# A turn of attention on one Trainium2 core: the order of a unit's scores, projections, sums and transpositions

## The chip, the cores and the metric

The kernel runs on one core of a Trainium2 chip. The core has a matrix engine (TensorE, PE in the profile; PEld are its weight loads), a vector engine (VectorE, DVE), an engine for activation functions (ScalarE, ACT), a general engine (GpSimd, POOL) and an engine that issues most of the copies (SyncE, SP). The engines run side by side; each works through its own queue in order, and semaphores make one wait for another. TensorE writes its results into PSUM, eight banks of 128 x 512 f32 numbers, and VectorE and ScalarE read them from there.

The metric is the device time of one launch in microseconds (us). The profile shows one execution, instruction by instruction. Its span is from the first to the last instruction.

## The reference

Three layers are computed on 16 batches of 512 tokens, 256 wide: half a feed-forward layer, an attention layer, half a feed-forward layer again, each added to its input. The change touches the attention layer alone:

```python
b, s, e = x.shape                        # 16, 512, 256; x is layer-normalized
q = x @ Wq + bq
kv = x @ Wkv + bkv
k, v = jnp.split(kv, [H * DQK], axis=-1) # H = 16 heads, DQK = DV = 64
q = _rope(q.reshape(b, s, H, DQK).transpose(0, 2, 1, 3))
k = _rope(k.reshape(b, s, H, DQK).transpose(0, 2, 1, 3))
scores = jnp.einsum('bhqd,bhkd->bhqk', q, k) * (1.0 / np.sqrt(DQK))
scores = jnp.where(causal[None, None], scores, -jnp.inf)
probs = jax.nn.softmax(scores, axis=-1)
out = jnp.einsum('bhqk,bhkd->bhqd', probs, v)
return out @ Wo + bo                     # heads beside each other again
```

All is f32.

## The kernel before

The program has three stages: the first feed-forward layer, attention, and the second feed-forward layer. Attention works on *units*: a batch and a group of four heads, 64 units in all, four to a batch. It is a loop over turns, `for u in range(-2, nu)`. A turn works on several units at once, each at another step: it makes q and k of unit u+3 (`queries_keys`), the scores and the softmax weights of unit u+2 (`new`), the values of unit u+1 (`values`, p_v), and the weighted sums (`sums`, p_av) and the output projection (`leave`, p_ay) of unit u. In this loop the queues of all engines hold the instructions in the order in which the program's lines issue them (`manual_schedule`). So the order of the calls is the order of the work.

The 512 tokens of a unit are four tiles of 128 queries. Tile i needs (i+1) x 128 keys, because of the causal mask. The steps:

- `Rotated.half` and `add`: p_q and p_k, each in two halves of 128 x 512. VectorE multiplies each half by the cosine and by the sine (four instructions for q, four for k), POOL adds and subtracts.
- `exps(tiles)`: scores p_as. Four heads stand in four groups of 32 rows of TensorE's array, and each head has a PSUM bank. VectorE reads each bank (L853: scale, mask and the row's minimum of the negated scores, amn), ScalarE exponentiates (L857) and sums the row (ars). Tile 3, tile 2, and tiles 1 and 0 together are three calls. Tiles 3 and 2 stand in the buffer pr0, tiles 1 and 0 in pr1.
- `normalize(tiles)`: VectorE's reciprocal of the sums (L862), then POOL scales the weights (L865).
- `turn_most(0..3)`, `turn_corner`, `turn_rest`: VectorE transposes the weights in blocks of 32 x 32 from pr into sq (L880), five instructions for tiles 3 and 2 and two for tiles 1 and 0.
- `move`: SP issues 16 copies of 160 KB (L903) from sq into prT, which put the blocks of 32 into the right partitions. sq and prT have one buffer each.
- `values`: p_v in two halves on the whole 128 x 128 array; ScalarE copies them out (L809).
- `sums`: p_av, two calls of two heads; each head uses 64 columns of the array. It reads prT. ScalarE copies the result out with a bias (oT, L940).
- `leave`: p_ay on the whole array, two calls; VectorE adds them to x (L953). After a batch's last head group SP copies x out.

At every fourth turn a new batch begins: `enter` normalizes its tokens on ScalarE (L759) and adds the output bias to x on POOL (L762), and `width` transposes them on TensorE (p_ahT, L769; ScalarE copies the two halves into ahT, L770), which p_q, p_k and p_v read. Once in two batches `spread` takes a square root on ScalarE, for which a table of functions is loaded and then the exponential's again.

TensorE's order in a turn before is: sums, (width), scores 3, p_v, p_q, scores 2, p_k, p_v, scores 1 and 0, p_ay. The four `turn_most` and the corner of a unit stand at the end of the turn that made its weights. `turn_rest` and the copies stand in the next turn, behind the sums.

All PSUM tiles take the eight banks in rotation: a tile waits until the one eight before it has been read.

## Time and profile before

| | us |
|---|---|
| median of 3 runs | 2398.57 |
| lowest and highest | 2395.6 and 2398.81 |
| the profiled execution | 2397.34 |
| its span | 2395.6 |
| attention in it | about 475 to 1994 |
| one turn, TensorE's sums to the next sums | 23.77; 24.80 where a batch begins |
| busy in one turn of 23.78: PE, DVE, ACT, POOL | 23.78, 20.42, 11.48, 13.15 |

A row of a group or of the timeline gives the start or the busy time in us, the engine, the line of the kernel, the operation, the output and inputs by their names in the program, and the number of instructions; what stands in brackets is the idle time before it and what ended it. In the chain, a row is the start, the length and the work that the end of the program had to wait for. Ends of matmuls are modelled in the profile, and neighbouring ones overlap by a little.

### The profile page before, as it was taken

Reading aid. Unit: us, or ns where it says so; the run is one execution under the profiler, and the core shown is the slowest. Engines: PE = TensorE matmul, PEld = TensorE weight load, DVE = VectorE, ACT = ScalarE, POOL = GpSimd, SP = SyncE. Lnnn points to the kernel's source line nnn. Section 1 sums busy time; section 2 is a strip of 40 time slices with the busy share of each in tenths; the row PEclk is TensorE's granted clock in tenths of the full one; section 3 lists DMA queues with packets and bytes.
Section 4 is the critical chain, followed back from the end, with each engine's and each line's share of the span. In section 5 each row is a group of like instructions: output and inputs, shape, how many; then the busy total and the mean of one; then the engine's idle time right before and its main releaser. Section 6 shows DMA issues by size and latency. Waiting matters only on the chain.

```text
span 2395.6 us, 42393 instructions
## 1 busy us (share of the span) xinstructions
PE 2334.5 (97%) x14696; PEld 1468.1 (61%) x14696; DVE 1771.7 (74%) x4669; ACT 1072.4 (45%) x2924; POOL 1067.4 (45%) x1692
## 2 busy tenths in 40 slices
PE   7999889899999999999999999999999999999899
PEld 5765479455565655555555555555555566765488
DVE  8542278788888888888888888888888865542287
ACT  4333233355455555545545545555555453323233
POOL 2220044555564655565646555556555542210043
PEclk9999999999999999999999999999999999999999
DMA  9009942245454545464645454646454545019734
GB/s 319 12 2 372 365 117 71 45 106 124 103 127 107 123 112 119 106 132 97 133 105 124 105 125 98 136 94 139 100 126 103 126 104 187 1 54 383 302 111 137
DMA packets 141709, 320.56 MB, mean 134 GB/s; under 512 B 36980, under 2 KB 84152, under 8 KB 133304
## 3 DMA queue, kind: packets, MB, share of 16 engines
q1 hardware_dynamic: 140908, 317.31, 49.7%
q8 instruction: 117, 1.92, 0.3%
q14 instruction: 96, 0.79, 0.1%
q10 hardware_dynamic: 588, 0.54, 0.1%
HBM read 135.84 MB, written 16.78 MB: 64 GB/s over the span
## 4 chain that ended last, share of the span: by engine, by line
PE 85%; DVE 3%; DMA 2%; ACT 2%; issue 1%; POOL 0%; SPq 0%; DVEq 0%; ACTq 0%; POOLq 0%
PE p_as L845 13%; PE p_av L933 12%; PE p_v L806 9%; PE p_ay L949 9%; PE p_k L784 9%; PE p_q L784 9%; PE p_cy L661 4%; PE p_cq L369 4%; PE p_cs L630 2%; PE p_z L480 2%; PE p_u L522 2%; PE p_ds L449 2%; DMA w<-in_e_Wg_dram 1%; PE p_catT L651 1%; PE p_y L549 1%; PE p_vw L619 1%
## 5 line engine op out<-in xcount | busy, mean ns | idle before, releaser
L865 POOL TENSOR_SCALAR pr<-pr,ars 128x512 f32<-128x512 f32 (+3 forms) x1024 | 525.0, 537 | 653.7 <-DVE ars L862 653.7
L857 ACT ACTIVATE pr<-pr,amn 128x512 f32<-128x512 f32 (+3 forms) x1024 | 561.5, 549 | 462.1 <-DVE amn L853 462.0
L853 DVE CUSTOM_DVE_ANT_0 pr<-p_as,causal 128x512 f32<-128x512 f32 (+3 forms) x1024 | 434.3, 484 | 97.8 <-PE p_as L845 96.3
L880 DVE STREAM_TRANSPOSE sq<-pr 128x768 f32<-128x768 f32 x441 | 375.7, 906 | 13.5 <-issue 12.3
L845 PE MATMUL p_as<-k,q 32*128 32x512 f32 (+3 forms) x4096 | 332.5, 449 | 3.6 <-POOL k L795 3.6
L933 PE MATMUL p_av<-prT,v 128*64 128x512 f32 (+3 forms) x2048 | 291.7, 438 | 7.2 <-DVE ars L862 6.3
L845 PEld LDWEIGHTS p_as<-k,q 32*128 32x128 f32 x4096 | 180.1, 185 | 131.8 <-issue 51.9
L806 PEld LDWEIGHTS p_v<-wv,ahT 128*128 128x128 f32 x1024 | 189.3, 190 | 98.5 <-issue 45.8
L806 PE MATMUL p_v<-wv,ahT 128*128 128x256 f32 x1024 | 248.4, 386 | 0.0
L933 PEld LDWEIGHTS p_av<-prT,v 128*64 128x64 f32 x2048 | 140.0, 137 | 164.8 <-issue 134.1
L949 PE MATMUL p_ay<-wo,aoT 128*128 128x256 f32 x1024 | 238.7, 386 | 0.3 <-ACT aoT L940 0.3
L784 PE MATMUL p_k<-ahT,wk 128*128 128x512 f32 x512 | 236.9, 605 | 0.0
L784 PE MATMUL p_q<-ahT,wq 128*128 128x512 f32 x512 | 230.5, 592 | 0.2 <-ACT ahT L770 0.2
L949 PEld LDWEIGHTS p_ay<-wo,aoT 128*128 128x128 f32 x1024 | 189.1, 190 | 32.0 <-ACT aoT L940 1.1
L857 ACT ACTIVATION_READ_ACCUMULATOR pr<-pr,amn 128x1 f32 x1024 | 191.4, 187 | 0.0
L784 PEld LDWEIGHTS p_k<-ahT,wk 128*128 128x128 f32 x512 | 92.1, 189 | 126.2 <-issue 115.9
L940 ACT ACTIVATE aoT<-p_av,bcol 128x512 f32<-128x512 f32 x128 | 88.0, 687 | 181.1 <-PE p_av L933 181.1
L784 PEld LDWEIGHTS p_q<-ahT,wq 128*128 128x128 f32 x512 | 97.1, 190 | 95.8 <-issue 86.6
L608 POOL TENSOR_TENSOR kbd<-kT,own 128x256 f32<-128x256 f32 x32 | 19.7, 619 | 290.1 <-DVE kT L575 253.0
L661 PE MATMUL p_cy<-vw,catT 128*128 128x256 f32 x512 | 122.7, 384 | 3.0 <-ACT catT L653 3.0
L480 PE MATMUL p_z<-atT,h 128*128 128x256 f32 x512 | 120.2, 389 | 3.9 <-ACT atT L471 3.9
L809 ACT COPY v<-p_v 128x512 f32<-128x512 f32 x128 | 73.5, 574 | 104.3 <-PE p_v L806 104.3
(157 smaller groups left out, 3292.0 us busy)
## 6 DMA issues: line engine op xcount, KB each, us to landing
prT<-sq SPq DMA_DIRECT2D x1008, 160.0 KB
w<-in_e_W_dram SPq DMA_DIRECT2D x64, 1024.0 KB
w<-in_e_Wg_dram SPq DMA_DIRECT2D x32, 1024.0 KB
out_dram<-x SPq DMA_DIRECT2D x64, 256.0 KB
xl<-in_attn_x_dram SPq DMA_DIRECT2D x16, 512.0 KB
xl<-out_dram SPq DMA_DIRECT2D x16, 512.0 KB
x<-in_attn_x_dram SPq DMA_DIRECT2D x15, 512.0 KB
wq<-in_attn_Wq_dram SPq DMA_DIRECT2D x16, 64.0 KB
```

Source lines behind the costliest of these rows:

```text
L369: nc.tensor.matmul(pq, w["c_Wq"][:, k, c * P:(c + 1) * P], hTs[b][:, k, :], start=(k == 0), stop=(k == NC - 1))
L480: nc.tensor.matmul(pz[:, c * 256:(c + 1) * 256], h[:, t, c * P:(c + 1) * P], atT[:, t, :], start=(t == 0), stop=(t == NT - 1))
L661: nc.tensor.matmul(py[:, t * D:(t + 1) * D], atT[:, c, t * P:(t + 1) * P], vws[b][:, c, :], start=(c == 0), stop=(c == NC - 1))
L784: nc.tensor.matmul(pq, self.w[:, k, at:at + P], hTs[self.b][:, k, :], start=(k == 0), stop=(k == NC - 1))
L806: nc.tensor.matmul(pv[:, t * 256:(t + 1) * 256], hTs[b][:, k, (t0 + t) * P:(t0 + t + 1) * P], wv[:, k, hg * HG * DQ:(hg + 1) * HG * DQ], s ...
L845: nc.tensor.matmul(banks[j][:, at:at + w], q[n][j * 32:(j + 1) * 32, i * P:(i + 1) * P], k[n][j * 32:(j + 1) * 32, :w], start=(n == 0), st ...
L853: nc.vector.tensor_tensor_reduce(out=self.at(i, j), in0=banks[j][:, at:at + w], in1=causal[:, S - w:], scale=-1.0 / math.sqrt(DQ), scalar= ...
L857: nc.scalar.activation(self.at(i, j), self.at(i, j), AF.Exp, bias=self.mn[:, i, j:j + 1], scale=-1.0, accum_out=self.rs[:, i, j:j + 1])
L865: nc.gpsimd.tensor_scalar(self.at(i, j), self.at(i, j), self.rs[:, i, j:j + 1], 1.0, ALU.mult, ALU.mult)
L880: nc.vector.transpose(view(self.sq, j * blocks * SQ + dst[0] * SQ, [(blocks * SQ, nh)] + [(s * SQ, n) for s, (_, n) in zip(dst[1:], of)] + ...
L933: nc.tensor.matmul(po[j * DQ:(j + 1) * DQ, :].rearrange("d (a f) -> d a f", a=NSQ)[:, :, t * SQ:], vs[u][:, t, head * DQ:(head + 1) * DQ], ...
L949: nc.tensor.matmul(py[:, t * D:(t + 1) * D], oTs[u][:, pair, (t0 + t) * P:(t0 + t + 1) * P], wo[:, hg * (HG // 2) + pair, :], start=(pair ...
```

## The change

Calls in the turn change their places; what is computed stays as it was.

- TensorE's order becomes: sums, scores 3, p_v, (width), p_v, p_q, p_k, p_ay, scores 2, scores 1 and 0. `queries_keys` is not cut in pieces any more, and `leave` comes before scores 2.
- VectorE turns a unit's weights in one go in the turn after the one that made them: `turn_most(0)`, the reciprocal of tiles 1 and 0, `turn_most(1..3)`, the corner and the rest, and then the copies are issued. The reciprocal of tile 2 stands halfway in the reads of tiles 1 and 0 (`halfway`).
- `enter` moves to the start of the turn that needs it, ahead of the sums; the addition of the output bias is split off (`with_bias`) and follows the scaling of tiles 1 and 0 on POOL.
- `width` moves from ahead of scores 3 to between the two halves of p_v.
- `spread` moves ahead of `leave` and scores 2.
- In the last turns of the loop the last unit's scaling and its transpositions on TensorE (`turn_at_once`) move likewise; `normalize` is called `scaled`.

```diff
+        def with_bias(b):
             for t in range(NT):
                 nc.gpsimd.tensor_tensor(xs[b][:, t, :], xs[b][:, t, :], row, ALU.add)
...
-            def exps(self, tiles):
+            def exps(self, tiles, halfway=None):
...
                 for j in range(HG):
+                    if halfway and j == HG // 2:
+                        halfway()
...
-            def normalize(self, tiles):
+            def scaled(self, tiles):
...
                 old = ws.get(u + 1)
-                if old and u + 2 == nu:
+                fresh = u + 3 < nu and units[u + 3][1] == 0
+                if fresh:
+                    enter(units[u + 3][0])
+                if u + 2 == nu:
+                    old.scaled((1, 0))
                     values(u + 1, 0)
                     values(u + 1, 2)
-                    old.turn_at_once()
                 if u >= 0:
                     sums(u, 0)
                     sums(u, 1)
-                if old and u + 2 < nu:
+                if old and u + 2 == nu:
+                    old.turn_at_once()
+                elif old:
+                    old.turn_most(0)
+                    old.scaled((1, 0))
+                    old.turn_most(1)
+                    old.turn_most(2)
+                    old.turn_most(3)
+                    old.turn_corner()
                     old.turn_rest()
                     old.move()
+                if fresh:
+                    with_bias(units[u + 3][0])
                 if u + 4 in stds:
                     scales((u + 4) // (PB * NHG), stds.pop(u + 4))
-                if u + 3 < nu and units[u + 3][1] == 0:
-                    width(units[u + 3][0])
                 if new:
                     new.exps((3,))
...
                 if new:
-                    new.normalize((3,))
+                    new.scaled((3,))
                 if 0 <= u + 1 < nu - 1:
                     values(u + 1, 0)
-                for one in qk[:2]:
+                if fresh:
+                    width(units[u + 3][0])
+                if 0 <= u + 1 < nu - 1:
+                    values(u + 1, 2)
+                for one in qk:
                     one()
+                if 0 <= u + 5 < nu and (u + 5) % (PB * NHG) == 0:
+                    stds[u + 5] = spread((u + 5) // (PB * NHG))
+                if u >= 0:
+                    leave(u, 0)
+                    leave(u, 2)
                 if new:
                     new.exps((2,))
-                for one in qk[2:3]:
-                    one()
-                if new:
-                    new.normalize((2,))
-                for one in qk[3:]:
-                    one()
-                if 0 <= u + 1 < nu - 1:
-                    values(u + 1, 2)
-                if 0 <= u + 5 < nu and (u + 5) % (PB * NHG) == 0:
-                    stds[u + 5] = spread((u + 5) // (PB * NHG))
-                if new:
-                    new.exps((1, 0))
-                if u >= 0:
-                    leave(u, 0)
-                if new:
-                    new.normalize((1, 0))
-                turns = new and u + 3 < nu
-                if turns:
-                    new.turn_most(0)
-                    new.turn_most(1)
-                if u >= 0:
-                    leave(u, 2)
-                if turns:
-                    new.turn_most(2)
-                    new.turn_most(3)
-                    new.turn_corner()
-                if u + 4 < nu and units[u + 4][1] == 0:
-                    enter(units[u + 4][0])
+                    new.exps((1, 0), lambda: new.scaled((2,)))
```

More of the change, by code (lines that the diff above doesn't have):

```diff
@@ L968, in attention @@
         enter(0)
+        with_bias(0)
         ap = yield [lambda: width(0)] + queries_keys(0)
```

## The prediction

> **What bounds the kernel now.** I read the page's first part, the chain, one turn in the chain's order of time, that turn on the other engines, and last a turn that was late.

> ```profile
> PE 2334.5 (97%) x14696; PEld 1468.1 (61%) x14696; DVE 1771.7 (74%) x4669; ACT 1072.4 (45%) x2924; POOL 1067.4 (45%) x1692
> ...
> PE 85%; DVE 3%; DMA 2%; ACT 2%; issue 1%; POOL 0%; SPq 0%; DVEq 0%; ACTq 0%; POOLq 0%
> ```

> TensorE is the bound. The attention stage (475 to 1994 us) is 64 units; its steady turns are nearly all TensorE:

> ```profile
> 1223.24 4.46 PE p_av L933 x32
> 1227.69 1.93 PE p_as L845 x16
> 1229.62 1.92 PE p_v L806 x8
> 1231.55 3.43 PE p_q L784 x8
> 1234.98 1.50 PE p_as L845 x16
> 1236.48 3.63 PE p_k L784 x8
> 1240.12 1.73 PE p_v L806 x8
> 1241.84 1.52 PE p_as L845 x32
> 1243.36 3.65 PE p_ay L949 x16
> ```

> See the same work at two prices: p_v 1.92 after scores, 1.73 after p_k; p_k 3.63 after scores, the same shape as p_q (3.43, after p_v); p_ay 3.65 after scores, as much as two p_v (3.46). About 0.2 us goes at each change between 32-row scores, 64-column sums and whole-array work. There are seven changes in a turn; a turn takes 23.77 us, one that starts a new batch (four more transposes to each half, p_ahT) 24.80. The clock is granted at 1.00 there.

> The other engines in that turn:

> ```profile
> 1223.78 0.20 DVE L862 RECIPROCAL ars<-ars 128x8 f32<-128x8 f32 x1 [1.26 <-ACT pr L857]
> 1226.87 4.13 DVE L880 STREAM_TRANSPOSE sq<-pr 128x768 f32<-128x768 f32 x5
> 1224.08 3.23 POOL L865 TENSOR_SCALAR pr<-pr,ars 128x256 f32<-128x256 f32 x8 [2.62 <-DVE ars L862]
> 1234.53 0.56 ACT L809 COPY v<-p_v 128x512 f32<-128x512 f32 x1
> ```

> VectorE's last transposition of a unit ends at 1231.0, 7.5 us after the sums began (1223.2); sixteen copies (sq to prT) follow, and the next sums need them all. How close that is shows in a turn after a square root (two table loads on ScalarE), where VectorE was 1.5 us later:

> ```profile
> 765.91 4.53 PE L933 MATMUL p_av<-prT,v 128*64 128x512 f32 x32
> 786.04 3.72 PE L949 MATMUL p_ay<-wo,aoT 128*128 128x256 f32 x16
> 790.04 2.23 PE L933 MATMUL p_av<-prT,v 128*64 128x512 f32 x13 [0.28 <-issue]
> 770.75 4.13 DVE L880 STREAM_TRANSPOSE sq<-pr 128x768 f32<-128x768 f32 x5
> ```

> The windows around its end (columns: stretch, its length, busy PE, PEld, DVE, ACT, POOL, clock, DMA share, GB/s):

> ```profile
> 789.00:789.50 0.50, 0.50 (x4) 0.33 (x2) 0.05 (x1) 0.50 (x4) 0.50 (x1) 1.00 0.05 21
> 789.50:790.00 0.50, 0.26 (x2) 0.00 (x0) 0.00 (x0) 0.50 (x3) 0.27 (x1) 1.00 0.00 0
> ```

> Transpositions end at 774.9, the copies move bytes until after 789.0, TensorE stands idle and starts at 790.04: 15.1 us after the last transposition. The chain names it "issue", but the copies are what it had to wait for. So the copies are hidden in an ordinary turn by little more than 1 us.

> **The change, step by step.**

> *Fewer changes of shape on TensorE.* A turn becomes sums, scores 3, then p_v, p_v, p_q, p_k, p_ay together, then scores 2 and 1/0 together. Three changes go: p_k at p_q's 3.43 (0.20), p_ay at 3.46 (0.19), scores 1/0 0.20 less (1.32; it has scores 2's column count, and no row shows it after scores, so I take the same 0.2; ends 0 and 0.24). TensorE's own turn: 4.46+1.93+1.92+1.73+3.43+3.43+3.46+1.50+1.32 = 23.18, that is 0.59 less. Over some 62 turns, 37 us, if nothing else waits.

> *What lies between a unit's last scores and its sums.* Before, from the end of scores 1/0 to the sums that need them there are p_ay and a whole turn, 3.65+23.77 = 27.4 us. After, p_ay has moved ahead of the scores, and only one turn is left: 23.18 us. What must pass in it, from the end of scores 2 (0): VectorE starts tile 2 at once, ScalarE 0.59 behind it (1213.23, 1213.82) and exponentiates four heads at a pitch of 0.60, so by 3.0 it takes tiles 1 and 0, now queued right behind; these take 3.62 (1220.13 to 1223.75): 6.65. VectorE has by then read them, done the reciprocal of tile 2 and turn_most(0) (about 5.7), and stands at the reciprocal of tiles 1/0, which waits for ScalarE. POOL begins 0.30 after that reciprocal and scales for 3.23: 10.3 with a handover. VectorE's other three turn_most and the corner (3×0.88+0.58) run beside it and are no later. The last two transpositions, which need POOL, take 1.8: 12.1. Scores 1/0 end 1.3 after scores 2, so the last transposition stands 10.8 us after the last scores. The nearest row is the chain of before, 11.1 (scores end 1195.7, transpositions 1206.9); bounds 10.0 (POOL's last heads overlap the first of the two) and 11.8 (VectorE late at the scores, and the 0.2 to 0.55 idle ahead of a first transposition on the path). With 15.1 of copies (the late turns, among them those that begin at 958.51 and 1536.33, show 14.9 to 15.3): 25.9 against a cover of 23.18. The sums are late by 2.72. turn_most(0) now also waits until the copies of the unit before have left sq, and all of VectorE's turn is queued behind it; they have landed when the late sums begin, 2.72 after the scores, and VectorE comes to it at about 3.6, so I take nothing for it (0.9 of cover; later copies would add their excess to the chain).

> The wait is shared by two turns: lateness of one start delays nothing in the chain measured from the scores before it. So two plain turns take 23.18+25.9 = 49.1 us, against 47.5 before.

> The late turn measured 15.1 us for the copies, at 205 to 208 GB/s. [...]

> *A new batch.* `width` moves from just after the sums to behind the first p_v; its two ScalarE copies (ahT) now stand behind the four exponentials of tile 3 and p_v's copy, and p_q needs them. The exponentials wait for VectorE to read scores 3, which stands behind all transpositions. Before: last transposition 1206.87, p_v's copy from 1210.40, 3.5 later; add 0.57 for it and 0.53 for the first ahT: 4.65 after the last transposition (two copies took 1.06). After, that is 10.8−2.72+4.65 = 12.7 from the start of the sums. TensorE is ready for p_q at 4.46+1.93+1.92+1.03+1.73 = 11.07. It waits 1.66 (bounds: 0, if ahT comes earlier than I think; 4.4, where the sums were not late).

> *The rest, at nothing.* enter stands ahead of the sums' evictions on ScalarE (2.06 us): TensorE doesn't need these banks until p_q. with_bias (2.8 us of POOL) follows the scaling, with POOL idle until tile 3's reciprocal; without that cover it would delay p_k's rotation. The square root and its table loads now stand ahead of p_ay, where ScalarE waits for scores 2 anyway; the late turns (0.24 and 0.36 us over; 1.0 the most) go, 2.4 us in all. p_ay's two adds on VectorE now stand ahead of its reads of scores 2; p_ay ends 1.5 before these do and an add takes 0.65, so they wait for nothing unless VectorE is behind (third rival). SP's queue: the outputs' copies stay behind the sixteen, none passes another, and the sixteen start after the sums' end at 4.5 as before. PSUM: p_k takes the banks of scores 3, the first two read by 11.5 and 12.1 of a turn; p_k starts at 13.5.

> *Sum.* Of four turns one starts a batch: 23.18+1.03+1.66 = 25.87; then no wait (the copies had time), a wait, none, a wait: a block is 25.87+25.9+23.18+25.9 = 100.85 us. Before: 24.80+3×23.77 = 96.11. 15 blocks × 4.74 = 71.1, less 2.4 = 69 us. The profiled execution took 2397.34 us (span 2395.6), 1.2 under the median of 2398.57: 2397.3+69 = 2466.

> **Rivals.** Under 0.2% (5 us) counts as no change.

> *TensorE never waits (faster).* Then 37+2.4 us go: 2358. For it: the 0.2 us are plain in the rows. It needs last transpositions no later than 8.1 after the scores for the copies, and 6.4 for ahT. Against it: ScalarE alone is busy until 5.35 after the scores, and POOL and VectorE follow by semaphore. The block breaks even where the last transposition comes 8.5 after the scores. I give 0.07, and 0.03 to no change.

> *One of the two waits isn't there.* Without ahT's wait, 15×1.66 = 25 less: 2441. With the chain at its lower bound, 10.0: 2×0.8×15 = 24 less: 2442; both: 2417. Chance 0.22.

> *VectorE becomes the bound.* It is busy 20.4 of 23.8 us, and now its reads of p_ay come just ahead of scores 2: stats, q, k and p_ay end at about 22 in a turn, when scores 2 end. Late by 1 us, or copies or chain at their upper ends (2×(1.0+0.2)×15 = 36): 2502. Chance 0.08.

> **How the numbers follow.** The forecast holds 0.60 between 2442 and 2500. 2466 is its value. Range 2417 to 2500: out go the faster and the equal case (0.10) and the part beyond 2500 (0.08). Slower in all but the first rival: 0.90; same 0.03; faster 0.07.

> **What would show it.** Right: TensorE idle some 2 to 3 us ahead of p_av in every second turn, or 1.4 in each; the last transposition 8 to 11 after the start of the sums; some 1.7 idle ahead of p_q in every fourth turn; p_k near 3.43 and p_ay near 3.46. Wrong: p_av back to back with the scores (the copies or the chain are shorter than taken), p_q waiting 4 us or not at all, or scores 2 waiting for banks (VectorE the bound).

## The result, and the profile after

The changed kernel takes 2484.76 us (median of 4 runs, 2475.49 to 2492.17), the kernel before beside it 2397.6 (4 runs, 2395.6 to 2398.81). The ratio is 1.036, with a 95% interval of 1.0325 to 1.040: 87 us slower. 2466 was forecast, with a range of 2417 to 2500. The profiled execution is the longest of the four, 2492.17 us with a span of 2490.4.

The page after, shares of the span by engine, and the head of the chain:

```profile
PE 2344.9 (94%) x14696; PEld 1519.3 (61%) x14696; DVE 1789.0 (72%) x4669; ACT 1049.7 (42%) x2924; POOL 1066.4 (43%) x1692
...
PE 72%; ACT 8%; DVE 6%; DMA 3%; SPq 2%; issue 2%; POOL 1%; DVEq 0%; ACTq 0%; POOLq 0%
```

TensorE was 85% of the chain, now it is 72%, and ScalarE (8%, it was 2%), VectorE and the copies have taken the rest. TensorE is busy 10 us longer than before (2344.9 us against 2334.5), and its idle time has grown by 84 us, from 61 to 146. Here is a turn that starts a batch and the plain one behind it, on TensorE (start, length, and in brackets the idle time before):

```profile
1219.41 4.53 PE L937 MATMUL p_av<-prT,v 128*64 128x512 f32 x32 [1.77 <-DVE ars L866]
1223.87 2.00 PE L847 MATMUL p_as<-k,q 32*128 32x512 f32 x16
1225.80 1.99 PE L808 MATMUL p_v<-wv,ahT 128*128 128x256 f32 x8
1227.63 1.04 PE L771 MATMUL p_ahT<-ident,h 128*128 128x128 f32 x8
1228.50 1.89 PE L808 MATMUL p_v<-wv,ahT 128*128 128x256 f32 x8
1232.44 3.70 PE L786 MATMUL p_q<-ahT,wq 128*128 128x512 f32 x8 [2.04 <-ACT ahT L772]
1235.98 3.60 PE L786 MATMUL p_k<-ahT,wk 128*128 128x512 f32 x8
1239.41 3.62 PE L953 MATMUL p_ay<-wo,aoT 128*128 128x256 f32 x16
1242.96 2.88 PE L847 MATMUL p_as<-k,q 32*128 32x384 f32 x48
1245.77 4.53 PE L937 MATMUL p_av<-prT,v 128*64 128x512 f32 x32
...
1271.50 4.53 PE L937 MATMUL p_av<-prT,v 128*64 128x512 f32 x32 [2.50 <-DVE amn L857]
...
1294.67 4.53 PE L937 MATMUL p_av<-prT,v 128*64 128x512 f32 x32
```

Both forecast gaps are there. The sums (p_av) of every second turn are late, by 1.77 and 2.50 here, and not those between (1245.77 and 1294.67 follow the scores at once). In a new batch's turn p_q waits 2.04 for ahT. The gain is there too: from 1271.50 to 1294.67 a turn without a wait takes 23.17 us, where 23.77 were needed.

The label of the gap ahead of p_av, "DVE amn", names the engine whose semaphore came last by the profile. What TensorE had to have are the copies; the chain has them ahead of the sums at 1271.50, until 1271.30:

```profile
1265.80 5.50 DMA prT<-sq
```

VectorE's rows of the turn from 1245.77, and the windows behind them (columns: stretch, length, busy PE, PEld, DVE, ACT, POOL, clock, DMA share, GB/s):

```profile
1251.20 0.20 DVE L866 RECIPROCAL ars<-ars 128x8 f32<-128x8 f32 x1 [1.36 <-ACT pr L861]
1251.32 4.96 DVE L884 STREAM_TRANSPOSE sq<-pr 128x768 f32<-128x768 f32 x6
```

```profile
1258.00:1268.00 10.00, 10.00 (x56) 6.31 (x58) 8.81 (x20) 2.84 (x8) 7.61 (x8) 1.00 0.98 217
...
1270.50:1271.00 0.50, 0.00 (x0) 0.00 (x0) 0.48 (x6) 0.50 (x3) 0.00 (x0) 1.00 0.03 10
1271.00:1271.50 0.50, 0.00 (x1) 0.03 (x1) 0.50 (x6) 0.50 (x3) 0.38 (x1) 1.00 0.00 0
```

The scores end at 1245.77, VectorE's last transposition at 1256.28, 10.5 us later (its reciprocal had waited for ScalarE, as the bracket says); bytes move until 1270.8, and the sums start at 1271.50, 15.2 us after that transposition.

### The profile page after: what moved, and what is told of

Its sections match the earlier page's. It is cut to its first block, busy times and chain, and to the rows that moved or that the text cites. A ratio compares the mean times of both kernels' runs of the same rounds, so it can differ in the third digit from the quotient of the medians.

```text
span 2490.4 us, 42410 instructions
## 1 busy us (share of the span) xinstructions
PE 2344.9 (94%) x14696; PEld 1519.3 (61%) x14696; DVE 1789.0 (72%) x4669; ACT 1049.7 (42%) x2924; POOL 1066.4 (43%) x1692
## 3 DMA queue, kind: packets, MB, share of 16 engines
q8 instruction: 117, 1.92, 0.3%
## 4 chain that ended last, share of the span: by engine, by line
PE 72%; ACT 8%; DVE 6%; DMA 3%; SPq 2%; issue 2%; POOL 1%; DVEq 0%; ACTq 0%; POOLq 0%
PE p_av L937 10%; PE p_as L847 8%; PE p_q L786 8%; PE p_ay L953 8%; PE p_k L786 8%; ACT pr L861 7%; PE p_v L808 6%; PE p_cy L661 4%; PE p_cq L369 4%; DVE sq L884 3%; PE p_cs L630 2%; PE p_z L480 2%; SPq L907 2%; PE p_ds L449 2%; PE p_u L522 2%
## 5 line engine op out<-in xcount | busy, mean ns | idle before, releaser
L857 DVE CUSTOM_DVE_ANT_0 pr<-p_as,causal 128x512 f32<-128x512 f32 (+3 forms) x1024 | 432.9, 483 | 41.2 <-PE p_as L847 40.6
L937 PE MATMUL p_av<-prT,v 128*64 128x512 f32 (+3 forms) x2048 | 326.8, 477 | 72.2 <-DVE amn L857 34.5
L847 PE MATMUL p_as<-k,q 32*128 32x128 f32 (+3 forms) x4096 | 318.1, 442 | 3.7 <-DVE k L792 3.4
L937 PEld LDWEIGHTS p_av<-prT,v 128*64 128x64 f32 x2048 | 165.6, 150 | 228.5 <-issue 128.4
L786 PE MATMUL p_q<-ahT,wq 128*128 128x512 f32 x512 | 234.7, 601 | 19.7 <-ACT ahT L772 19.7
L847 PEld LDWEIGHTS p_as<-k,q 32*128 32x128 f32 x4096 | 192.6, 185 | 97.1 <-issue 46.5
L808 PE MATMUL p_v<-wv,ahT 128*128 128x256 f32 x1024 | 240.6, 386 | 0.0
L953 PE MATMUL p_ay<-wo,aoT 128*128 128x256 f32 x1024 | 231.8, 379 | 0.2 <-ACT aoT L944 0.2
L786 PE MATMUL p_k<-ahT,wk 128*128 128x512 f32 x512 | 230.4, 592 | 1.3 <-DVE amn L857 1.3
L953 PEld LDWEIGHTS p_ay<-wo,aoT 128*128 128x128 f32 x1024 | 194.4, 190 | 53.0 <-issue 24.1
L608 POOL TENSOR_TENSOR kbd<-kT,own 128x256 f32<-128x256 f32 x32 | 19.7, 619 | 288.4 <-DVE kT L575 252.0
L792 DVE SCALAR_TENSOR_TENSOR q<-p_q,bcol,cos 128x512 f32<-128x512 f32 x128 | 94.5, 738 | 64.0 <-PE p_q L786 63.9
L957 DVE TENSOR_TENSOR x<-p_ay,x 128x512 f32<-128x512 f32 x128 | 85.3, 686 | 49.0 <-PE p_ay L953 49.0
```

The source lines that it names most:

```text
L786: nc.tensor.matmul(pq, self.w[:, k, at:at + P], hTs[self.b][:, k, :], start=(k == 0), stop=(k == NC - 1))
L808: nc.tensor.matmul(pv[:, t * 256:(t + 1) * 256], hTs[b][:, k, (t0 + t) * P:(t0 + t + 1) * P], wv[:, k, hg * HG * DQ:(hg + 1) * HG * DQ], s ...
L847: nc.tensor.matmul(banks[j][:, at:at + w], q[n][j * 32:(j + 1) * 32, i * P:(i + 1) * P], k[n][j * 32:(j + 1) * 32, :w], start=(n == 0), st ...
L857: nc.vector.tensor_tensor_reduce(out=self.at(i, j), in0=banks[j][:, at:at + w], in1=causal[:, S - w:], scale=-1.0 / math.sqrt(DQ), scalar= ...
L937: nc.tensor.matmul(po[j * DQ:(j + 1) * DQ, :].rearrange("d (a f) -> d a f", a=NSQ)[:, :, t * SQ:], vs[u][:, t, head * DQ:(head + 1) * DQ], ...
L953: nc.tensor.matmul(py[:, t * D:(t + 1) * D], oTs[u][:, pair, (t0 + t) * P:(t0 + t + 1) * P], wo[:, hg * (HG // 2) + pair, :], start=(pair ...
```

## The experiments

The theory: the sums wait for the sixteen copies, because p_ay no longer lies between a unit's last scores and its sums; p_q waits for ahT, whose copies stand behind tile 3's exponentials on ScalarE. Rivals: VectorE, or its turning of the weights at one go, or the long stretch of whole-array work costs by itself. A further question came from the profile after: the sums that follow a gap are at times slow (6.2 us in place of 4.5). All times below are medians; the kernel before took 2396.1 to 2396.5 us beside them.

### width back ahead of scores 3

```diff
+                if fresh:
+                    width(units[u + 3][0])
                 if new:
                     new.exps((3,))
...
-                if fresh:
-                    width(units[u + 3][0])
```

> The changed kernel (2485 us) with width put back ahead of scores 3, the rest as changed. Two-waits theory (the sums wait for the copies, and in every fourth turn p_q waits for ahT): only the second wait goes, 2.0 us in 15 turns, so about 2455 (2445 to 2465); TensorE still stands 2 to 3 us ahead of p_av in every second turn. If VectorE's queue is the bound, p_q's wait is only slack and the time stays at 2475 to 2490.

Measured: 2460.1 us, 25 less than the changed kernel. p_q's wait is gone from the list of waits, the sums' is there:

```profile
PE p_av L937 <- DVE amn L857: 32.4, 14, 2.8
PE p_av L937 <- DVE ars L866: 28.8, 14, 2.2
```

So p_q's wait was on the path, and VectorE was not behind it. In the profile of the changed kernel this wait comes to 19.7 us in all, in the run's time it was worth 25, where 30 were expected.

### p_ay back behind the last scores

```diff
-                if u >= 0:
-                    leave(u, 0)
-                    leave(u, 2)
                 if new:
                     new.exps((2,))
                     new.exps((1, 0), lambda: new.scaled((2,)))
+                if u >= 0:
+                    leave(u, 0)
+                    leave(u, 2)
```

> The changed kernel with p_ay (leave) put back behind scores 1/0, the rest as changed: one change of shape more (23.38 us for TensorE's own turn), and 3.65 us more between the last scores and their sums, 27.0 in all against the 25.9 that chain and copies need. Two-waits theory: no wait ahead of p_av any more, p_q's wait 0.7, the clock stays granted at 1.00: 2383 (2375 to 2395), faster than before. If VectorE turning a unit's weights at one go, or its load, is what costs, the time stays above 2440.

Measured: 2397.6 us, 1.0005 of the kernel before (0.9996 to 1.0015). The sums wait no more (but for 1.9 us in the loop's last turn), p_q's wait has shrunk to 0.28, and with that 87 us are gone: the place of p_ay decides. But the 13 us of gain that were expected didn't come. A plain turn takes 23.70 us, not 23.38; the next run shows why.

### Both

The two edits above together.

> Both of these put back: width ahead of scores 3 and p_ay behind scores 1/0; what is left of the change is the whole-array work in one stretch up to p_k, scores 2 and 1/0 together, and VectorE's order. Two-waits theory: neither wait, 5 changes of shape in place of 7, 62 turns of about 23.4 us: 2373 (2365 to 2385). If the longer stretch or VectorE's order costs by itself: 2400 or over.

Measured: 2387.8 us, 0.9962 of before (0.9947 to 0.9977). 0.4% faster than before, with the long stretch and with VectorE's order as changed, so neither is what the 87 us went into. The chain of this run, one plain turn's scores 2 and 1/0:

```profile
1186.47 3.14 PE p_as L847 x46
```

In the changed kernel the same work takes 2.81 where it doesn't wait (the 2.88 of the timeline at 1242.96, less the overlap). 0.33 us more in 62 turns are 20 us, enough for the 15 that were missing in the last run and here.

### Half of the copies

```diff
-                    for q in range(NSQ):
+                    for q in range(NSQ if self.u < 1 else NSQ // 2):
```

(prT is one tile for all units here, so that the rows that aren't copied hold older weights.)

> The changed kernel with only 8 of the 16 copies of each unit after the first (the sums then read old weights for half of the rows; that part is left out). Copies theory: 8 copies take some 8 us, the sums are never late, p_q's wait grows to about 4.4 in every fourth turn because the turn is no longer late at its start: 2425 (2415 to 2450, the upper end if these longer waits halve the clock). If VectorE or the chain ahead of the copies is the bound rather than the copies: 2470 to 2485.

Measured: 2451.9 us, just past the upper end. No sums wait any more; what is left is p_q's wait, and it has grown:

```profile
PE p_q L786 <- ACT ahT L772: 56.1, 14, 4.1
```

```profile
1208.24 1.04 PE L771 MATMUL p_ahT<-ident,h 128*128 128x128 f32 x8
...
1214.89 5.40 PE L786 MATMUL p_q<-ahT,wq 128*128 128x512 f32 x8 [3.88 <-ACT ahT L772]
```

So the copies are the path to the sums, and the one wait had hidden part of the other: a turn that starts late gives ScalarE time. p_q's work after this gap takes 5.40 us in place of 3.70, with the clock granted at 0.50 from 1216 to 1218. All 15 turns that start a batch have such a stretch (the mean granted clock of this run is 0.976, that of the kernel before 0.990); at some 2 us each they make up the difference between the 2425 expected and the time measured. The transpositions p_ahT don't wait here, though the sums are on time.

### VectorE's part alone

On the kernel before: the four turn_most and the corner move from the end of a turn to the next one, behind the sums, ahead of turn_rest.

```diff
                 if old and u + 2 < nu:
+                    for j in range(HG):
+                        old.turn_most(j)
+                    old.turn_corner()
                     old.turn_rest()
...
-                turns = new and u + 3 < nu
-                if turns:
-                    new.turn_most(0)
-                    new.turn_most(1)
                 if u >= 0:
                     leave(u, 2)
-                if turns:
-                    new.turn_most(2)
-                    new.turn_most(3)
-                    new.turn_corner()
```

> The kernel before with one part of the change alone: VectorE turns a unit's weights at one go in the next turn, behind the sums; TensorE's order, width and p_ay as before. In-order theory: VectorE's queue runs in order, so which turn the calls are written in moves them by little; only p_ay's second add now comes ahead of all of them, and the chain stays near 11.1 us with 27.4 us of cover: 2397 (2390 to 2405). If turning at one go is what costs: above 2420.

Measured: 2394.4 us, 0.9992 of before (0.9982 to 1.0002). "At one go" is worth nothing either way.

### The gap filled

On the changed kernel, two matmuls that nobody needs in the gap ahead of the late sums (four rows in the trace):

```diff
                     new.exps((1, 0), lambda: new.scaled((2,)))
+                if u >= 2 and u % 2 == 0 and u + 3 < nu:
+                    pf = ps(f"p_fill{u}")
+                    for n in range(2):
+                        nc.tensor.matmul(pf, wq[:, 0, n * P:(n + 1) * P], hTs[units[u + 3][0]][:, 0, :],
+                                         start=True, stop=True)
```

> The changed kernel with two matmuls more (128x512 on the whole array, 1.7 us, their result is read by nobody) behind scores 1/0 of every even turn, where TensorE stands 2.1 to 2.5 us. Clock theory: the idle time halves the granted clock for 3.4 us about 20 times in attention (71.7 us at 0.5, about 36 us lost); with the gap filled these stretches go and the time falls by 25 to 40 us, to 2445 to 2460. If the slow sums that follow a gap have another cause (the copies writing prT, say), the time stays at 2475 to 2490 or rises.

Measured: 2470.9 us, 14 less than the changed kernel, by added work. That lies between the two ranges, so the clock's rows have to decide. This is what the fill acts on, in the changed kernel: the sums behind one such gap, beside those behind none, and the clock in three windows (the last column but two):

```profile
1169.29 6.22 PE L937 MATMUL p_av<-prT,v 128*64 128x512 f32 x32 [2.13 <-DVE ars L866]
...
1194.15 4.53 PE L937 MATMUL p_av<-prT,v 128*64 128x512 f32 x32
```

```profile
1168.00:1169.20 1.20, 0.00 (x0) 0.00 (x0) 1.18 (x10) 1.20 (x5) 0.00 (x0) 1.00 0.00 0
1169.30:1171.00 1.70, 1.70 (x8) 0.73 (x10) 1.70 (x9) 1.70 (x9) 1.70 (x4) 0.88 0.00 0
1171.00:1173.00 2.00, 2.00 (x12) 1.32 (x10) 0.65 (x3) 1.79 (x9) 0.74 (x2) 0.50 0.00 0
```

No copy moves a byte in these windows, so the slow sums are not a collision with the copies; the granted clock is 0.50. With the fill, TensorE's gap is 0.35 and the clock stays at 1.00 (1209 to 1213):

```profile
1206.59 1.98 PE L1037 MATMUL p_fill<-ahT,wq 128*128 128x512 f32 x4
1208.92 4.53 PE L937 MATMUL p_av<-prT,v 128*64 128x512 f32 x32 [0.35 <-DVE amn L857]
```

By the clock's records in the trace the changed kernel has 20 stretches at 0.50 in attention ahead of the last two turns, 3.4 or 6.8 us each, the filled one 4; the mean granted clock is 0.973 and 0.988. The cause holds; the size (25 to 40 us) was taken too high. 7 of the 20 fall into turns that start a batch: there the slow sums only shorten p_q's wait. 12 fall into plain turns, which take 24.7 to 24.9 us in place of 23.17, and cost 20 us. One follows p_q's wait in the first turn that starts a batch, in both kernels. The other three of the filled kernel follow p_q's wait too, in turns of 28.2 us in place of 26.2, and cost 6: 20 less 6 are the 14.

### Neither wait

width ahead of scores 3, as in the first run, and half of the copies, as above.

> The changed kernel without either wait: width ahead of scores 3 and 8 of the 16 copies (half of the weights' rows are old; that part is left out). What is left is the saving by fewer changes of shape. Two-waits theory: every turn takes TensorE's own 23.2 us, the clock stays at 1.00, 0.6 us less in some 62 turns: 2358 (2353 to 2368), the time of the first rival. If the long stretch has a cost of its own, or VectorE is the bound at this pace: 2380 or over.

Measured: 2406.4 us. The number falls into the range of the rival, but the rows don't bear it out: the plain turns take 23.17 us, as expected (the seven behind a square root 23.4), so the long stretch has no cost of its own, and VectorE keeps up with this pace. But a turn that starts a batch takes 26.5 to 28.5, where TensorE's own work is 24.2, because a third wait comes up:

```profile
1185.01 0.33 PE L771 MATMUL p_ahT<-ident,h 128*128 128x128 f32 x1 [1.14 <-ACT h L759]
...
1184.37 2.06 ACT L759 ACTIVATE h<-x,shift,rstd 128x256 f32<-128x256 f32 x4
```

The normalized tokens h come from `enter`, which stands behind the exponentials of the turn before; these end some 5 us after the scores. If width stands ahead of scores 3, the sums aren't late and p_ay isn't behind the scores, nothing covers it; with width behind the first p_v, as in the run with half of the copies, p_ahT came some 3.8 us later and had no such wait. In 6 of the 15 such turns the clock drops as well (scores 3 at 1089.21 take 3.62 us, at 1187.18 2.00; the run's mean granted clock is 0.987). 15 turns with some 3.2 us too much are 48 us: the difference from 2358.

### Tile 3's scaling later

Towards a faster kernel. Both edits, and on POOL the scaling of tile 3 behind the rotation of q and k:

```diff
-                if new:
-                    new.scaled((3,))
...
                 for one in qk:
                     one()
+                if new:
+                    new.scaled((3,))
```

> width ahead of scores 3 and p_ay behind scores 1/0, as in the run with both put back (2388), and POOL's scaling of tile 3 moved behind the rotation of q and k. There scores 2 and 1/0 took 3.14 us where TensorE alone needs 2.81: scores 1/0 wait for the banks of p_k, which VectorE reads late because it may not write before POOL has added q, and POOL was scaling tile 3. If that is the cause, 0.33 us go in 62 turns: 2368 (2362 to 2375), faster than both kernels. If the banks wait for VectorE's own load: 2385 to 2390.

Measured: 2390.8 us, 0.9975 of before (0.9964 to 0.9986), no faster than without it; scores 2 and 1/0 still take as long (3.21 in the timeline, 3.14 without the overlap). POOL is not what VectorE waits for:

```profile
1237.12 3.21 PE L847 MATMUL p_as<-k,q 32*128 32x384 f32 x48
...
1237.30 0.75 DVE L792 SCALAR_TENSOR_TENSOR k<-p_k,bcol,sin 128x512 f32<-128x512 f32 x1 [0.38 <-PE p_k L786]
1237.97 0.74 DVE L792 SCALAR_TENSOR_TENSOR k<-p_k,bcol,cos 128x512 f32<-128x512 f32 x1
```

VectorE waits for TensorE to end p_k, reads it twice, and is done at 1238.7, but the first scores of tiles 1/0 are due at 1238.5 and one head's bank is this one.

### p_q and p_k ahead of p_v

Both edits, and in the stretch:

```diff
+                for one in qk:
+                    one()
                 if 0 <= u + 1 < nu - 1:
                     values(u + 1, 0)
                     values(u + 1, 2)
-                for one in qk:
-                    one()
```

> width ahead of scores 3 and p_ay behind scores 1/0, as in the run with both put back (2388), and p_q and p_k now ahead of p_v in the whole-array stretch. Scores 1/0 take the banks of the four tiles of that stretch that were written last; with p_k last its second half is read by VectorE only 1.5 us after TensorE ends it, about 0.3 us after scores 1/0 want the bank. With p_v last, ScalarE copies the last bank out in 0.6 us. Bank theory: scores 2 and 1/0 fall from 3.14 to 2.81 us and a plain turn from 23.70 to 23.38: 2368 (2362 to 2375). If the 0.3 us have another cause than the bank: 2385 to 2390.

Measured: 2373.6 us, 0.991 of before (0.9892 to 0.9925); the kernel before took 2396.15 beside it. 22.6 us faster than the kernel before, 111 faster than the changed one. The chain of this run:

```profile
1188.21 4.46 PE p_av L937 x32
1192.67 1.93 PE p_as L847 x16
1194.60 3.63 PE p_q L786 x8
1198.22 3.43 PE p_k L786 x8
1201.66 3.45 PE p_v L808 x16
1205.11 2.81 PE p_as L847 x48
1207.92 3.65 PE p_ay L953 x16
1211.57 3.48 PE p_av L937 x21
```

Scores 2 and 1/0 are back at 2.81, a plain turn is 23.36 us (1188.21 to 1211.57), all on TensorE, with five changes of shape. Only the turn behind a square root still has scores of 3.1 (seven of them, 0.3 us each): 2 of the 5.6 us by which the time stays above 2368.

## Why the prediction was right, and by how much it was off

- *Fewer changes of shape.* Right, to the hundredth: 23.17 us for TensorE's own turn where 23.18 was summed. p_k and p_ay came out at the prices of p_q and two p_v, and scores 2 and 1/0 at 2.81 (1.50+1.32).
- *The sums wait for the copies.* Right, and its mechanism was shown from both sides: more cover (p_ay behind the scores) and shorter copies (half of them) each end it. The term was somewhat too large. The last transposition came 10.5 us after the scores, not 10.8, and the late sums in the trace total 65.3 us, 30 of them, 2.18 each where 2.72 was taken: 16 us too much.
- *Every second turn.* Right: 1245.77 and 1294.67 are on time, 1219.41 and 1271.50 late.
- *p_q waits for ahT.* Right; 2.04 us in the turn shown, and 26.25 us for such a turn on average against the 24.2 of its work, 2.05, where 1.66 was taken: 6 us too little. In 7 of these turns the slow sums stand in place of most of the wait (0.4 us of it or less is left); with the gaps filled, the wait is 1.8 us on average. Without the late start it grew to 3.9, near the 4.4 given as the upper bound.
- *At nothing.* p_ay's adds, enter, with_bias and SP's queue cost nothing visible in the changed kernel. But the text named nothing that covers enter; the run with neither wait shows its price, 2.3 us and more in a new batch's turn, as soon as width stands ahead of scores 3. In the changed order width stands late enough.
- *The first rival's 2358.* It failed by its own condition: the last transposition had to come 8.1 us after the scores, and came 10.5 after. The run with neither wait took 2406, because the cure for the second wait brought up the third.
- *VectorE.* Its tie with scores 2 is real: in the seven turns behind a square root scores 2 and 1/0 take 3.13 in place of 2.88 (1214.51). It is a quarter of a microsecond, not the bound.
- *What the sum lacked.* The clock. The prediction noted that it was granted at 1.00 in attention, and then summed with gaps in TensorE's work as if it stayed there. In the profiled run 12 plain turns lost some 1.67 us each, 20 us. That is about the difference between the forecast, 2466, and the median, 2485; with the gaps filled the time was 2471. That the forecast came so near is in part luck: the late sums were taken 16 us too long, which made up for most of the clock.
- *A reading.* By its own rows the last transposition of before ends 7.8 us after the sums began (1223.24 to 1231.00), not 7.5, so that the copies were hidden by about 0.9 us. No term of the sum rests on it.

In the profiled execution the 15 blocks of four turns (from the second sums, 501.73, to 2032.15) take 102.0 us each, 96.3 before (501.08 to 1945.17), where 100.85 was forecast. By terms, in us over all of them: shape −36 (forecast −35), late sums +65 (+82), ahT +31 (+25), clock +20 (0), and the late turns behind square roots, gone, −2.4 (−2.4). That is 78 of the 86 measured. The first of these turns takes 31.02 us, 5 more than its like: its sums are on time, so that p_q waits 4.13, and the clock is at 0.50 for 6.8 us. The rest, some 3 us, is not traced. Between the two whole executions lie 95 us; most of the other 9 come from the loop's last turn, 15.2 us in place of 8.5, where the sums wait 3.6 us for the copies and the clock falls again.

## What to carry to other kernels

For every value that is made in one turn and used in a later one, count what the bound engine has to do between the two, before and after a move: here a reorder that saved 0.6 us a turn cut the cover by 4.2 us (27.4 to 23.2), and it had had about 1 us to spare. Grouping like work pays only as far as each group's results leave the array in time, so the last tiles written ahead of a group that needs their banks should be those that are read fastest (here scores 2 and 1/0 took 3.14 us behind p_k, whose last half VectorE reads in 1.4, and 2.81 behind p_v). When a wait is removed, look at once for the next one behind it: late starts had covered a part of ahT's wait, and moving width ahead to end that wait brought up the one for h.

## What the runs showed of the hardware

```profile
1167.17:1170.58 3.41, 1.29 (x8) 0.66 (x10) 3.39 (x22) 3.41 (x15) 1.30 (x3) 1.00 0.17 32
1170.59:1174.00 3.41, 3.41 (x16) 1.73 (x14) 2.06 (x4) 2.57 (x11) 2.15 (x5) 0.50 0.03 5
...
1269.57:1272.98 3.41, 1.48 (x8) 0.75 (x10) 3.39 (x20) 3.41 (x16) 1.86 (x4) 1.00 0.03 8
1272.99:1276.40 3.41, 3.41 (x30) 2.08 (x30) 2.06 (x5) 2.24 (x9) 2.15 (x6) 1.00 0.00 0
```

The gap of 2.13 lies in one window, the longer one of 2.50 in two. Of the windows at full clock in the changed kernel's attention, ahead of the last two turns, all 17 with 2.0 us of idle time or more were followed by the slow clock, and none with 1.7 or less; of the 12 with 1.84 to 1.99, three were. The longest idle time in one of these windows is 2.73 us. In the run with neither wait the clock fell after windows with as little as 1.2 to 1.7 us of idle time, in which the single transpositions p_ahT stand (the longest wait ahead of one is 1.4 us); why is open.

The four runs of the changed kernel differ by 16.7 us (those of the kernel before by 3.2), and with the mean clock: 2473.7 us of span at 0.981, 2490.4 at 0.973. That fits gaps that fall differently on the grid from run to run, but only one of these runs has a trace.

Sixteen copies of 160 KB within the chip's memory took 14.9 to 15.3 us from the last transposition to the sums. In the turn shown their bytes move from 1257.5 to 1270.8, 1.2 us after the transposition and 0.7 ahead of the sums: 2.62 MB at some 200 GB/s. In the run with half of the copies the last byte of the eight came 7.9 us after the transposition.
